# Order of the 64-row products in a four-layer graph network: lower rows first, then upper rows

## The chip, the core and the metric

The kernel runs on one core of a Trainium2 chip. A core has five engines with an instruction queue each: PE (TensorE, matrix products), DVE (VectorE), ACT (ScalarE), POOL (GpSimd) and SP (SyncE, which here only issues DMA transfers). They run side by side and wait for each other through semaphores. The metric is the device time of one execution in microseconds (us), lower is better.

## What is computed

The reference is four message-passing layers over one graph with 8,192 nodes, 32 features a node and 262,144 edges that are sorted by their target node. Each layer adds its result to the features and normalizes every node.

```python
x = layernorm(x + L0(x))     # msg = x[src] @ weight[edge_type]          (64 weights of 32x32)
x = layernorm(x + L1(x))     # msg = x[src] * edge_weight
x = layernorm(x + L2(x))     # msg = x[src]
x = layernorm(x + L3(x))     # h = relu(edge_attr_32 @ W1 + b1); w = h @ W2 + b2   (256 numbers an edge)
                             # msg = tensor product of x[src], edge_attr_4 and w
# in each layer: out = segment_sum(msg, dst)
```

## The kernel before

`raw_layers` writes its own order: each engine's instructions stand in the order of the Python loops, and waits are written out (`PE.after(mark)` makes PE's queue wait for a mark of another engine; `X.mark(ins)` sets one). No scheduler moves anything.

**Layer 0** first makes the table of x times all 64 weights in DRAM (L475). Then a loop over 256 groups `g` of 1,024 edges follows. POOL gathers the table rows of the edges, eight indirect DMAs a group, from `fetch_rows` through `indirect` (L454); it is let up to twelve groups ahead of PE (`AHEAD = 12`): the first half of group g+12 waits for PE's sums of g, the second half for all that PE has been given in g by then. DVE builds a one-hot matrix and splits the rows into three bfloat16 parts (`pairs`, `parts`; its first wait for a gather is at L858, its last step L863). PE then sums the group by target (L897).

In the same loop the kernel prepares layers 1 and 2: `matrices(i)`, 256 calls, 56 of the groups 8 to 207 with two calls and the others with one. Each call counts, for 128 nodes, which source blocks their edges come from, with and without the edge weight. DVE makes the one-hot operands `oh_k` and `oh_l` (L638, L640, L643) in two buffers, so that DVE's call i waits for PE's call i-2 (`oh_used`). PE then runs four rounds `q` of eight products (L654), and ACT empties each round with two copies (L658, L659). A round has its own two PSUM banks out of two pairs, so that round q waits for ACT's copies of round q-2 (`pair_free`). The operands of each product fill 64 of the 128 partitions: h = 0 the lower half, h = 1 the upper one. PE works with the rows of its array that belong to these partitions. The two halves write different PSUM banks.

The groups also run the first products of layer 1 (`layer1`, `products`, L717) as soon as counts and normalized nodes are there; `plan()` fixes at build time how many go into which group. None are planned before group 38. In the groups 8 to 207 it places 168; 100 of these 200 groups, 70 of the 170 from group 38 on, have none. `turn_back` (L736) and `add_up` (L752) finish a finished block of them; `normalize` with `windows` (L575) runs in groups 37, 69, 101, 133, 165, 197 and later ones.

**Layers 1 and 2** then run on the stored counts without gathers (L717, L1033).

**Layer 3** is a loop over 512 quads `q` of 512 edges. POOL gathers four times a quad, up to eight quads ahead (the gather of quad q+8 waits for PE's L1211 of quad q). PE's queue holds, for each quad: every second time the hidden layer (L1170, 32 rows), four products `h @ W2` (L1211, 64 rows each, added to biases that ACT wrote at L1190), and the summing of quad q-4 by target (L1221). DVE forms the messages (L1235 to L1256). Of the four products, `t` = 0 and 1 use the lower 64 rows and the first PSUM bank, `t` = 2 and 3 the upper rows and the second bank.

Every float32 product shows up in the profile as two weight loads and two passes: L654 has 256 x 4 x 8 = 8,192 products and 16,384 matmul records.

Of the kernel before, what the change touches and what calls it, by code (L numbers as in the profile page):

```python
# [161 lines left out]
def in_order(ctx: ExitStack, tc, x, a, w0, w1, b1, w2, si, keep):  # L162
# [36 lines left out]
    with tc.tile_critical():  # L199
        raw_layers(tc, x, a, w0, w1, b1, w2, si, m, bad)  # L200
# [3 lines left out]
def raw_layers(tc, x, a, w0, w1, b1, w2, si, m, bad):  # L204
# [35 lines left out]
    def now(f):  # L240
        return (f.sem, f.n)

    def own(f, ins):

        mk = f.mark(ins)
        f.after(mk)
        return mk
# [383 lines left out]
    def matrices(i):  # L631

        b, pp, k0 = i % 2, i // 2, 16 * (i % 2)
        if i % WB == 0:
            V.after(now(V))
            own(V, V.e.tensor_copy(w_ps, meta_w.rearrange("p n k -> p (n k)")[:, i * 16:(i + WB) * 16]))
        V.after(oh_used[b])
        own(V, V.e.tensor_tensor(oh_k[:, b, :, 0, :], iota2[:, None, 0:64, 0].to_broadcast([P, 16, 64]),  # L638
                                 meta_k[:, pp, k0:k0 + 16, None].to_broadcast([P, 16, 64]), op=OP.is_equal))
        V.e.tensor_tensor(oh_l[:, b], iota2[:, None, :, 0].to_broadcast([P, 16, P]),  # L640
                          meta_l[:, pp, k0:k0 + 16, None].to_broadcast([P, 16, P]), op=OP.is_equal)
        wo = (i % WB) * 16
        vm = V.mark(V.e.tensor_tensor(oh_k[:, b, :, 1, :], oh_k[:, b, :, 0, :],  # L643
                                      w_ps[:, wo:wo + 16, None].to_broadcast([P, 16, 64]), op=OP.mult))
        PE.after(vm)
        for q in range(4):
            u = units[0] % 2
            units[0] += 1
            PE.after(pair_free[u])
            two = bank[:, 2 + 2 * u:4 + 2 * u, :]  # L650
            for j in range(4):
                for h in range(2):
                    hs_ = slice(64 * h, 64 * h + 64)
                    ins = PE.e.matmul(two[:, h].rearrange("p (c s j) -> p c s j", s=64, j=4)[:, :, :, j],  # L654
                                      oh_l[hs_, b, 4 * q + j, :], oh_k[hs_, b, 4 * q + j], start=True, stop=True)
            pm = PE.mark(ins)
            A.after(pm, st_ld[b].mark() if q == 0 and st_ld[b].n else None)
            A.e.activation(st_c[:, b, q], two[:, :, 0:256], AF.Copy)  # L658
            pair_free[u] = am = A.mark(A.e.activation(  # L659
                st_a[:, b, :, q].rearrange("p z h w -> p h z w"),  # L660
                two[:, :, 256:512].rearrange("p h (z w) -> p h z w", w=32), AF.Copy))
        oh_used[b] = pm
        S.after(am)
        st_ld[b].add(S.e.dma_start(amat[i // 128][i // 8 % 16, :, 0:P * 2048].rearrange("z (p w) -> p z w", w=2048)[:, :, 256 * (i % 8):256 * (i % 8 + 1)],
                                   st_a[:, b].rearrange("p z q h w -> p z (q h w)")))
        stored[i] = st_ld[b].add(S.e.dma_start(cmat[i], st_c[:, b].rearrange("p u h c -> p (u h c)")))
# [174 lines left out]
    def fetch_rows(g, h, let):  # L841

        if g < GG:
            G.after(let)
            gathers(ytab, row, g * GT // WT, g * GT % WT + h * GT // 2, GT // 2)
            if h == 1:
                landed[g] = under_way[-1]
# [30 lines left out]
    for g in range(GG + 2):  # L878
# [9 lines left out]
        h, bk, c = g % NO, (g // per) % 2, g % per  # L888
# [13 lines left out]
        if g >= FIRST:  # L902
            upto = min(CB, (g - FIRST + 1) * CB // SP1)
            while made < upto:
                matrices(made)
                made += 1
# [293 lines left out]
    for q in range(NQ + LAG3 + 2):  # L1200
# [5 lines left out]
            hidden(q + 2)  # L1206
        if q < NQ:
            PE.after(quad[q]["h"], bm)
            for t in (0, 2, 1, 3):
                hp, c0 = slice(32 * (t & 2), 32 * (t & 2) + 64), 256 * (q % 2) + t % 2 * P  # L1210
                ins = PE.e.matmul(wp[:, t, :], hs[hp, q // 2 % 2, c0:c0 + P], w2_s[hp], start=False, stop=True,  # L1211
                                  skip_group_check=True)
            quad[q]["w"] = PE.mark(ins)
            quad[q]["k"] = k, wp
            fetch_rows(q + AHEAD)
# [545 lines left out]
```

## Time and profile before

| what | value |
|---|---|
| median of 14 runs | 5785.61 us (5780.81 to 5790.93) |
| the profiled execution | 5787.71 us, of which its span 5785.9 us |
| layer 0's table, until the first gather at 223.0 | 223 us |
| layer 0's gathers, 2,048, first to last start | 223.0 to 2803.6 us |
| `matrices` on PE (L654), first to last start | 359.9 to 2401.9 us |
| layers 1 and 2 on PE after the loop | about 2804 to 3186 us |
| layer 3's gathers, 2,048, first to last start | 3169.1 to 5738.9 us |
| `h @ W2` (L1211), first to last start | 3186.4 to 5752.5 us |
| mean granted PE clock over the span | 0.87 of full |

How to read it: the page gives each engine's busy time, then the span in 40 slices with the busy share in tenths, then groups of instructions with their count, busy time, mean duration and the idle time before them with what ended it. PE's row counts matmul passes, PEld the loads of weights that run beside them. PEclk is the clock that the throttle granted to PE, in tenths. A busy engine is not the one that sets the end unless somebody waits for it; the ends of matmuls are modelled, their starts are recorded.

### The profile page before, as it was taken

How to read it: one execution, taken by the hardware profiler on the slowest of the kernel's cores; microseconds unless marked ns; L12 is line 12 of the kernel's file. 1: busy time of each engine (PE TensorE's matmuls, PEld its weight loads, DVE VectorE, ACT ScalarE, POOL GpSimd, SP SyncE). 2: the span in 40 equal slices, each digit the busy share in tenths (PEclk: the TensorE clock that was granted, in tenths of full speed). 3: DMA queues.
4: the chain of work that ended last, by engine and by line, in shares of the span. 5: the costliest groups of instructions: out<-in, count | busy, mean ns of one | idle time of the engine just before them, and what ended most of it. 6: DMA issues, size and time to landing. Idle time of an engine off the chain costs nothing.

```text
span 5785.9 us, 89563 instructions
## 1 busy us (share of the span) xinstructions
PE 4549.5 (79%) x34750; PEld 2971.7 (51%) x34750; DVE 4399.7 (76%) x9506; ACT 2229.9 (39%) x3323; POOL 4141.7 (72%) x4236
## 2 busy tenths in 40 slices
PE   7456777778778788654599888889898888889897
PEld 3146666666666666432355444444444444444454
DVE  4269898989989898443355778878788878878786
ACT  5255555555555555210177222222222222222222
POOL 2677777777777777777356777777777777777775
PEclk7578888989999899756589899999999999999899
DMA  9636667769788899955576111111111111111111
GB/s 349 217 103 209 183 211 229 250 226 325 248 298 309 276 347 324 348 178 190 193 253 215 26 26 30 26 30 30 26 30 26 30 30 26 30 26 30 26 30 22
DMA packets 583331, 865.52 MB, mean 150 GB/s; under 512 B 102640, under 2 KB 441840, under 8 KB 549360
## 3 DMA queue, kind: packets, MB, share of 16 engines
q1 hardware_dynamic: 448320, 782.88, 38.5%
q0 software_dynamic: 134144, 73.67, 8.0%
q8 instruction: 276, 4.52, 0.3%
q10 hardware_dynamic: 432, 3.15, 0.2%
q14 instruction: 159, 1.30, 0.1%
HBM read 454.48 MB, written 404.88 MB: 149 GB/s over the span
## 4 chain that ended last, share of the span: by engine, by line
PE 18%; POOL 13%; DVE 8%; DMA 7%; issue 5%; ACT 1%; POOLq 0%; DVEq 0%
POOL f_arena L454 13%; DMA f_arena<-fxtab,f_src 7%; PE bank L1221 7%; PE bank L1033 4%; PE bank L1211 3%; DVE f_arena L1256 2%; PE bank L1170 1%; PE bank L717 1%; DVE f_arena L1252 1%; DVE f_arena L588 1%; ACT bank L1190 1%; PE bank L575 1%; PE bank L980 1%; DVE f_arena L1249 1%; DVE f_arena L1240 1%
## 5 line engine op out<-in xcount | busy, mean ns | idle before, releaser
L454 POOL DMA_INDIRECT f_arena<-fytab,f_row x2048 | 1957.7, 956 | 651.8 <-issue 549.5
L454 POOL DMA_INDIRECT f_arena<-fxtab,f_src x2048 | 1947.0, 951 | 643.4 <-issue 523.2
L654 PE MATMUL bank<-f_arena 64*128 64x128 f32 x16384 | 1208.7, 305 | 401.8 <-DVE f_arena L643 269.4
L1221 PE MATMUL bank<-f_arena 128*128 128x344 f32 x4096 | 1407.7, 488 | 0.0
L654 PEld LDWEIGHTS bank<-f_arena 64*128 64x128 f32 x16384 | 1111.2, 211 | 482.9 <-DVE f_arena L643 293.8
L1190 ACT ACTIVATE bank<-f_arena 128x1024 f32<-128x1024 f32 x512 | 526.5, 1029 | 1446.5 <-DVE f_arena L1256 1441.7
L1221 PEld LDWEIGHTS bank<-f_arena 128*128 128x128 f32 x4096 | 781.0, 201 | 531.0 <-issue 220.1
L658 ACT ACTIVATE f_arena<-bank 128x512 uint8<-128x512 f32 x1024 | 613.0, 599 | 844.9 <-PE bank L654 726.8
L1211 PE MATMUL bank<-f_arena 64*128 64x256 f32 x4096 | 621.4, 424 | 277.4 <-ACT bank L1190 276.7
L1211 PEld LDWEIGHTS bank<-f_arena 64*128 64x128 f32 x4096 | 370.8, 195 | 653.4 <-ACT bank L1190 471.3
L659 ACT ACTIVATE f_arena<-bank 128x512 f32<-128x512 f32 x1024 | 611.8, 597 | 0.0
L640 DVE TENSOR_TENSOR f_arena<-bank,f_arena 128x2048 f32<-128x2048 bf16 x256 | 586.6, 2291 | 8.7
L1256 DVE TENSOR_TENSOR f_arena<-bank,f_arena 128x256 f32<-128x256 f32 x1536 | 550.5, 413 | 0.0
L1134 DVE TENSOR_TENSOR f_arena<-f_arena 128x192 f32<-128x192 f32 x256 | 93.9, 367 | 396.9 <-DMA f_arena<-fxtab,f_src 395.8
L897 PE MATMUL bank<-f_arena 128*128 128x96 bf16 x2048 | 152.9, 227 | 305.8 <-DVE f_arena L863 305.8
L717 PE MATMUL bank<-f_arena,f_x_b 128*32 128x256 f32 x4096 | 327.3, 461 | 78.0 <-DMA f_arena<-famat 60.3
L588 DVE TENSOR_TENSOR f_arena<-bank,f_rel 128x512 f32<-128x512 f32 x512 | 348.6, 681 | 0.0
L1252 DVE TENSOR_TENSOR f_arena<-bank,f_arena 128x512 f32<-128x512 f32 x512 | 348.5, 681 | 0.0
L638 DVE TENSOR_TENSOR f_arena<-bank,f_arena 128x1024 f32<-128x1024 bf16 x256 | 312.0, 1219 | 15.1 <-PE bank L654 13.0
L897 PEld LDWEIGHTS bank<-f_arena 128*128 128x128 bf16 x2048 | 111.5, 108 | 388.9 <-DVE f_arena L863 299.4
L643 DVE TENSOR_TENSOR f_arena<-f_arena,bank 128x1024 f32<-128x1024 f32 x256 | 309.6, 1209 | 0.0
L1177 ACT ACTIVATE f_arena<-bank,f_arena 128x512 f32<-128x512 f32 x256 | 174.1, 680 | 336.6 <-PE bank L1170 336.3
(149 smaller groups left out, 4608.1 us busy)
## 6 DMA issues: line engine op xcount, KB each, us to landing
famat<-f_arena SPq DMA_DIRECT2D x256, 1024.0 KB
f_arena<-famat SPq DMA_DIRECT2D x256, 1024.0 KB, 6.6
fytab<-f_arena SPq DMA_DIRECT2D x64, 1024.0 KB, 11.9
fcmat<-f_arena SPq DMA_DIRECT2D x256, 256.0 KB
f_arena<-fcmat SPq DMA_DIRECT2D x16, 4096.0 KB, 14.7
f_arena<-fytab,f_row POOLq DMA_INDIRECT x2048
f_arena<-fxtab,f_src POOLq DMA_INDIRECT x2048
f_arena<-laid_ea SPq DMA_DIRECT2D x64, 512.0 KB
```

Source lines behind the costliest of these rows:

```text
L454: return G.e.indirect_dma_start(out=dest, out_offset=None, in_=table, in_offset=bass.IndirectOffsetOnAxis(ap=ix, axis=0))
L588: return V.e.tensor_tensor(o, iota[:, None, :].to_broadcast([P, n, P]), rel[:, t:t + n, None].to_broadcast([P, n, P]), op=OP.is_equal)
L640: V.e.tensor_tensor(oh_l[:, b], iota2[:, None, :, 0].to_broadcast([P, 16, P]), meta_l[:, pp, k0:k0 + 16, None].to_broadcast([P, 16, P]), o ...
L654: ins = PE.e.matmul(two[:, h].rearrange("p (c s j) -> p c s j", s=64, j=4)[:, :, :, j], oh_l[hs_, b, 4 * q + j, :], oh_k[hs_, b, 4 * q + j ...
L658: A.e.activation(st_c[:, b, q], two[:, :, 0:256], AF.Copy)
L659: pair_free[u] = am = A.mark(A.e.activation(st_a[:, b, :, q].rearrange("p z h w -> p h z w"), two[:, :, 256:512].rearrange("p h (z w) -> p ...
L717: ins = PE.e.matmul(acc[q * D:(q + 1) * D, :].rearrange("p (u h j) -> p u h j", h=2, j=4), x_b[:, 8 * z + s, :], mv[:, s], start=(first an ...
L1190: return A.mark(A.e.activation(wp, b2_s[:, None, :].to_broadcast([P, 4, 256]), AF.Copy))
L1211: ins = PE.e.matmul(wp[:, t, :], hs[hp, q // 2 % 2, c0:c0 + P], w2_s[hp], start=False, stop=True, skip_group_check=True)
L1221: ins = PE.e.matmul(bank[:, g % 2, 0:MW], oh[:, c % NO, t, :], p[:, c % NP, t, :], start=(c % 2 == 0 and t == 0), stop=(c % 2 == 1 and t = ...
L1252: V.e.tensor_tensor(pq[:, :, 0:128].rearrange("p t (o k) -> p t o k", k=16), wp[:, :, 0:128].rearrange("p t (o k) -> p t o k", k=16), a0[: ...
L1256: ins = V.e.tensor_tensor(pq[:, :, 128 + 64 * mm:192 + 64 * mm].rearrange("p t (o i) -> p t o i", i=8), wp[:, :, 192:256].rearrange("p t ( ...
```

## The change

Both places keep the same products, operands and PSUM banks; only their order on PE's queue differs. In `matrices`, the loop over the halves becomes the outer one: the four products on the lower 64 rows run first, then the four on the upper 64. In layer 3 the order of the four products goes from lower, upper, lower, upper to lower, lower, upper, upper.

```diff
@@ matrices
-            for j in range(4):
-                for h in range(2):
+            for h in range(2):
+                for j in range(4):
                     hs_ = slice(64 * h, 64 * h + 64)
                     ins = PE.e.matmul(two[:, h].rearrange("p (c s j) -> p c s j", s=64, j=4)[:, :, :, j],
                                       oh_l[hs_, b, 4 * q + j, :], oh_k[hs_, b, 4 * q + j], start=True, stop=True)
@@ layer 3
             PE.after(quad[q]["h"], bm)
-            for t in (0, 2, 1, 3):
+            for t in range(4):
                 hp, c0 = slice(32 * (t & 2), 32 * (t & 2) + 64), 256 * (q % 2) + t % 2 * P
                 ins = PE.e.matmul(wp[:, t, :], hs[hp, q // 2 % 2, c0:c0 + P], w2_s[hp], start=False, stop=True,
                                   skip_group_check=True)
```

## The prediction

> **What bounds the kernel now.** I read the page's engine rows and slices first, then the groups, then for both loops a stretch of the timeline in order of time.
>
> ```profile
> span 5785.9 us, 89563 instructions
> PE 4549.5 (79%) x34750; PEld 2971.7 (51%) x34750; DVE 4399.7 (76%) x9506; ACT 2229.9 (39%) x3323; POOL 4141.7 (72%) x4236
> ...
> PEclk7578888989999899756589899999999999999899
> ...
> L454 POOL DMA_INDIRECT f_arena<-fytab,f_row x2048 | 1957.7, 956 | 651.8 <-issue 549.5
> L454 POOL DMA_INDIRECT f_arena<-fxtab,f_src x2048 | 1947.0, 951 | 643.4 <-issue 523.2
> L654 PE MATMUL bank<-f_arena 64*128 64x128 f32 x16384 | 1208.7, 305 | 401.8 <-DVE f_arena L643 269.4
> ```
>
> The two gather streams set both loops: 2,048 gathers at 0.956 us plus some 0.3 us of issue are 2,580 us each, and the first runs from 223.0 to 2803.6, the second from 3169.1 to 5738.9. Mean spacing is 1.26 us, so POOL gives 10.0 us to a group of layer 0 (eight gathers) and 10.0 us to two quads of layer 3. PE, DVE and ACT follow it with some idle time. So the change costs what PE cannot hide under 10.0 us a group or a pair of quads.
>
> Where PE stands in the loops:
>
> ```profile
> 1254.89 2.14 PE L654 MATMUL bank<-f_arena 64*128 64x128 f32 x32 [0.29 <-ACT f_arena L659]
> 1256.97 0.51 PE L897 MATMUL bank<-f_arena 128*128 128x96 bf16 x8
> 1257.65 2.06 PE L654 MATMUL bank<-f_arena 64*128 64x128 f32 x32 [0.16 <-DVE f_arena L643]
> ```
>
> ```profile
> 4580.49 2.59 PE L1221 MATMUL bank<-f_arena 128*128 128x344 f32 x8
> 4583.01 1.07 PE L1170 MATMUL bank<-f_arena 32*64 32x512 f32 x4
> 4584.01 1.13 PE L1211 MATMUL bank<-f_arena 64*128 64x256 f32 x8
> 4585.08 2.59 PE L1221 MATMUL bank<-f_arena 128*128 128x344 f32 x8
> 4587.59 1.13 PE L1211 MATMUL bank<-f_arena 64*128 64x256 f32 x8
> 4588.66 2.59 PE L1221 MATMUL bank<-f_arena 128*128 128x344 f32 x8
> ```
>
> The reader is to see that 32 passes of L654 (two rounds) take 2.06 us although one pass lasts 0.27: a lower and an upper pass start 7 ns apart and run together, and the next pair starts 0.112 us later (0.213 at half clock). Rounds follow each other at 0.995 us, at half clock at 1.71. In layer 3 one L1211 block holds PE for 1.07 us, again in pairs (0.213 us each), and a pair of quads takes 4588.66 - 4580.49 = 8.17 us when PE never waits.
>
> **The clock.** The slices show it at 7 to 9 tenths. What it follows can be read in stretches:
>
> ```profile
> core 0: us, PE busy (x), PEclk, DMA share, GB/s
> 357.30:364.10 6.80, 4.21 (x38) 0.50 0.10 13
> 364.10:374.30 10.20, 7.01 (x109) 1.00 0.50 145
> 36.60:60.40 23.80, 22.90 (x72) 0.50 1.04 389
> 111.70:118.50 6.80, 6.80 (x34) 1.00 0.84 302
> 3186.00:5786.00 2600.00, 2273.07 (x9338) 0.94 0.15 28
> ```
>
> The two stretches at 36.60 and 111.70 hold only L475: passes of 32 rows and 512 columns. In both PE looks busy throughout, yet the first stays at half clock. A pass at full clock streams its 512 columns in 512/128 x 0.107 = 0.43 us (0.112 less 5 ns of start) on 32/128 of the array. So the array's work is 72 x 0.43 / 4 / 23.8 = 0.33 of its capacity in the first, 34 x 0.43 / 4 / 6.8 = 0.54 in the second. Weighted this way, by rows and columns in use, the clock's steps (3.4 us long) over the whole trace divide at about 0.37: steps below it are followed by half clock, steps above it by full clock, with some ten exceptions in 1,680. By time busy alone the L475 rows contradict. That matters here: alternating, L654 has work 0.107/0.112 = 0.96 at full and 0.49 at half clock, so it lifts the clock by itself (364.10 above). With one half at a time it has about half of that.
>
> **The change, part by part.** No instruction is added or removed; waits, banks and DMAs stay. What goes is the overlap of the halves.
>
> *One round of L654.* [...] Before, 8 pairs span 7 pitches; after, 14. Added: 7 x 0.112 = 0.78 us (1.49 at half clock). A round takes 1.78 (3.20), more than ACT's two copies at 0.60 each, so ACT stops ending PE's waits. A call of four rounds takes 7.1 us on PE at full clock, 13.0 at half (12.8 and 0.2 to start).
>
> [...]
>
> *Its work rate.* 16 passes x 0.107 x 1/2 = 0.85 us of the whole array in 1.78 us is 0.48; at half clock, in 3.20 us, 0.27. At full clock that stays above 0.37 if PE idles less than 0.8 us of a 3.4 us step. At half clock it can't climb; only full-array work in the same step can, of which products L717 (0.97 us each, near 0.9 of the array) are the supply: some 2 us of them at half clock must fall into one step.
>
> *Layer 0, groups 8 to 37* (355 to 658 us, 303 us; 38 calls). No L717 is planned and the clock is at half on entry. I expect it stays there: 38 x 13.0 + 30 x (0.82 for L897 + 0.3) = 528 us: **+225**. Bound below: full clock, 38 x 7.1 + 30 x 0.8 = 294, hidden: 0.
>
> *Groups 38 to 207* (658 to 2404 us, 1,746 us; 218 calls, 168 products). At full clock: 218 x 7.12 = 1,552; 168 x 0.97 = 163; 170 sums x 0.52 = 88; 106 turns (L736) x 0.63 = 67; five normalizations x 10 (6.5 us waiting for L863, and L575) = 50. PE has 1,920 us of work: **+174**, since POOL's 10.0 us a group no longer covers it.
>
> *Half clock in those groups.* Every group at half costs 1.28 calls x 5.9 + 0.6 = 8.1 us more. 70 of the 170 groups have no product to lift the clock; waits that drop it (five normalizations, 34 waits of ACT L658 for a store of `fcmat`) remain. I take 45 groups: **+366**. Bounds: 0, and all 170, +1,380.
>
> *What POOL's lead gives back.* At group 208 PE is now 70 us behind the gathers (2404 against 2335). It can be 12 groups x 10.3 = 123 us: 54 us are absorbed, **-54**. Groups 208 to 255 stay at POOL's pace, as before.
>
> *Queued behind it.* ACT's L658 and DVE's L638 (`oh_used`) wait for L654, and POOL's second half group for all of PE's calls; DVE has at most two calls of one-hots ready, so it slows to PE's pace but adds nothing: 9.4 us a group (3.2 for L583 and the parts, 1.28 x 4.7, 0.14).
>
> *Layer 3.* Four pairs (3 pitches) become 6 pitches: 3 x 0.213 = 0.64 us a quad; a pair of quads 8.17 + 1.28 = 9.45 us under POOL's 10.0, still covered. What isn't: eight normalizations keep PE from quads for some 14 us each, and the clock is at half for 336 of 2,600 us, which costs PE 168 us. 256 x 9.45 + 8 x 14 = 2,531, with those 168 us 2,699, against 2,570: between 0 and +130. Half-clock steps come from idle steps, which get fewer as PE fills: **+40**.
>
> **Sum:** 225 + 174 + 366 - 54 + 40 = 751 over the span of 5785.9 (its execution 5787.7, within 0.04% of the median 5785.6): **6537 us**.
>
> **Rivals.**
> *The clock stays up* (the gate counts time busy, or 0.48 is enough everywhere). [...] For it: L475 at 111.70 keeps full clock at 0.54. Against: 36.60. Terms: 0 + 174 + 0 - 54 + 20 = +140: 5926 us.
> *The clock stays down nearly everywhere.* For: once down, L654 can't lift it. Against: 100 groups with products. 225 + 174 + 1,380 - 54 + 130 = +1,855: 7641 us. With three quarters of the groups, 7296.
> *Not slower.* Gathers hide it all. PE's call would have to take at most (1,746 + 54 - 368) / 218 = 6.6 us, a round 1.64 instead of 1.78, so one pair in six would still have to overlap, and the clock to stay up. Then 5786 within 10. [...]
>
> **How the numbers follow.** Forecast 0.68, clock up 0.12, clock down nearly everywhere 0.15, not slower 0.05. The forecast's own range is 6170 (no half groups from 38 on) to 7000 (100 of them). For 8 in 10 the range goes from 5950, inside the first rival, to 7350, inside the second. A measurement tells about 0.2% (12 us) from no change: faster 0.02, same 0.03, slower 0.95.
>
> **What would show it.** L654 passes in one half 0.112 us apart, a round of 1.78 or 3.20 us; groups 8 to 37 at clock 0.5 taking some 530 us; half clock in layer 0 rising from 443 us to near 1,000; POOL waiting for L654; layer 3's gathers still near 2,570 us. Wrong if the clock in layer 0 stays near 0.9, if a round stays near 1.0, or if layer 3 grows by more than 130.

## The result, and the profile after

The changed kernel takes 5838.79 us (median of 6 runs, 5836.31 to 5844.52), the kernel before 5784.9 (28 runs): a ratio of 1.0094, 95% interval 1.0084 to 1.0104, some 54 us slower. The forecast was 6537, with a range from 5950: the sign was right, the size was not. The profiled execution of the changed kernel is 27 us above its median (5865.5, span 5863.7), so its differences to the trace before add up to 78 us, not 54.

From the page of the changed kernel:

```profile
span 5863.7 us, 89563 instructions
PE 4870.1 (83%) x34750; PEld 3315.3 (57%) x34750; DVE 4399.7 (75%) x9506; ACT 2270.0 (39%) x3323; POOL 4150.6 (71%) x4236
...
PEclk7578998989889899866579899999999999999998
...
L454 POOL DMA_INDIRECT f_arena<-fytab,f_row x2048 | 1960.7, 957 | 718.2 <-issue 549.5
L454 POOL DMA_INDIRECT f_arena<-fxtab,f_src x2048 | 1952.8, 954 | 643.4 <-issue 520.6
L654 PE MATMUL bank<-f_arena 64*128 64x128 f32 x16384 | 1542.9, 300 | 189.9 <-DVE f_arena L643 115.0
```

L654 is busy 334 us longer (1208.7 before), and idle 212 us less ahead of it (401.8). POOL's first gather stream idles 66 us more (651.8), the second not at all: the loss lies in layer 0. The slices show no fall of the clock. Stretches of PE in layer 0, groups 8 to 37 and 38 to 207, first before, then after (columns: stretch, length, PE busy, clock, DMA share, GB/s):

```profile
355.00:658.00 303.00, 207.54 (x2680) 0.84 0.61 185
658.00:2404.00 1746.00, 1347.85 (x18542) 0.90 0.83 278
```

```profile
357.00:663.00 306.00, 258.58 (x2688) 0.87 0.60 183
663.00:2501.00 1838.00, 1619.80 (x18526) 0.93 0.79 264
```

The clock is a little higher than before, the groups from 38 on take 92 us more. What one round costs now shows in the timeline of the changed kernel; before, the same 32 passes took 2.06 us:

```profile
1202.63 2.82 PE L654 MATMUL bank<-f_arena 64*128 64x128 f32 x32 [0.17 <-DVE f_arena L643]
```

By their recorded starts at full clock, a round's first upper pass begins together with the fifth of the eight lower passes, 0.55 us after the first, and its last upper pass 1.44 us after the first lower one (0.89 before). Where nothing holds the next round, it does not wait for that last pass: its first lower pass starts together with the fifth upper pass, ahead of the three upper ones that are left, 1.11 us after the first lower pass of the round before (0.995 in the kernel before; 1.78 forecast). The third round waits for ACT's copies of the first and begins 1.45 us after the first round's last pass in both kernels. As that pass now comes later, the third round begins 2.88 us after the first (2.35 before).

A call of four rounds lasts 5.70 us at full clock instead of 4.49 (7.1 forecast). Of these 1.21 us, 0.11 each lie between the starts of the first and second and of the third and fourth round, 0.43 between those of the second and third, and 0.56 in the last round itself.

Summed over the 256 calls that is 1331 us before and 1612 after, 281 more. In the groups 8 to 207 (2049 us before, 2144 after) the time outside the calls falls from 718 to 532: 186 of the 281 us went into time in which PE had waited anyway, 95 remained. At group 208 PE is 146 us behind the gathers instead of 69. POOL's lead hides little of this in the end: PE comes to group 208 97 us later than before, and the last gather of layer 0 starts 71 us later. Who waited for L654 in the changed kernel, in us and times:

```profile
  ACT f_arena L658: 819.3, 566
  POOL f_arena L454: 70.9, 74
```

POOL waited 20.4 us before: of the 71 us, 50 are POOL standing at the gate to the next group because PE had not got through its calls. POOL's waits from 2345 us on, when it fetches group 208 (total, times, longest):

```profile
POOL f_arena L454 <- PE bank L654: 35.0, 7, 12.5
POOL f_arena L454 <- PE bank L897: 20.6, 9, 11.8
```

No gather of layer 0 starts over 1.5 us after the one before it ended in the kernel before. In the changed kernel ten do: two in groups 177 and 180, 15 us together, and eight in groups 209 to 222, 52 us together. So the loss comes out where POOL reaches its gate.

Layer 3 of the changed kernel:

```profile
4304.57 1.07 PE L1170 MATMUL bank<-f_arena 32*64 32x512 f32 x4
4305.57 1.14 PE L1211 MATMUL bank<-f_arena 64*128 64x256 f32 x8
4306.64 2.59 PE L1221 MATMUL bank<-f_arena 128*128 128x344 f32 x8
```

L1211 holds PE for 1.07 us, as before. The starts of its eight passes (0, 13, 321, 333, 538, 551, 753, 766 ns) are nearly those of the alternating order (0, 6, 321, 326, 538, 544, 753, 759): with two products to a half, the upper half begins 13 ns after the lower one.

### The profile page after: what moved, and what is told of

The parts are those of the page before. It is cut to its first block, busy times and chain, and to the rows that moved or that the text cites. A ratio compares the mean times of both kernels' runs of the same rounds, so it can differ in the third digit from the quotient of the medians.

```text
span 5863.7 us, 89563 instructions
## 1 busy us (share of the span) xinstructions
PE 4870.1 (83%) x34750; PEld 3315.3 (57%) x34750; DVE 4399.7 (75%) x9506; ACT 2270.0 (39%) x3323; POOL 4150.6 (71%) x4236
## 4 chain that ended last, share of the span: by engine, by line
PE 16%; POOL 13%; DVE 8%; DMA 7%; issue 5%; ACT 1%; POOLq 0%; DVEq 0%
POOL f_arena L454 13%; DMA f_arena<-fxtab,f_src 7%; PE bank L1221 6%; PE bank L1033 4%; PE bank L1211 3%; DVE f_arena L1256 2%; PE bank L1170 1%; DVE f_arena L1252 1%; DVE f_arena L588 1%; ACT bank L1190 1%; PE bank L717 1%; PE bank L980 1%; PE bank L575 1%; DVE f_arena L1249 1%; DVE f_arena L1240 1%
## 5 line engine op out<-in xcount | busy, mean ns | idle before, releaser
L654 PE MATMUL bank<-f_arena 64*128 64x128 f32 x16384 | 1542.9, 300 | 189.9 <-DVE f_arena L643 115.0
L654 PEld LDWEIGHTS bank<-f_arena 64*128 64x128 f32 x16384 | 1452.3, 201 | 261.0 <-DVE f_arena L643 127.5
L658 ACT ACTIVATE f_arena<-bank 128x512 uint8<-128x512 f32 x1024 | 611.7, 597 | 916.5 <-PE bank L654 819.3
L1211 PE MATMUL bank<-f_arena 64*128 64x256 f32 x4096 | 618.1, 420 | 284.8 <-ACT bank L1190 284.1
L1211 PEld LDWEIGHTS bank<-f_arena 64*128 64x128 f32 x4096 | 377.7, 194 | 652.8 <-ACT bank L1190 482.3
L659 ACT ACTIVATE f_arena<-bank 128x512 f32<-128x512 f32 x1024 | 606.3, 592 | 0.0
L643 DVE TENSOR_TENSOR f_arena<-f_arena,bank 128x1024 f32<-128x1024 f32 x256 | 309.6, 1210 | 0.0
```

The lines of the kernel that those rows point to most:

```text
L659: pair_free[u] = am = A.mark(A.e.activation(st_a[:, b, :, q].rearrange("p z h w -> p h z w"), two[:, :, 256:512].rearrange("p h (z w) -> p ...
```

## The experiments

The question was why the halves still overlap, and where the 54 us come from. The theory after the result (A) was my reading of the starts in the changed kernel's trace: the upper half begins with the fifth of eight lower passes in L654 and with the first of four in L1211, so each time three lower passes still wait; if that is the most that can, only a run of more than four passes on one half loses anything. The expectations below give 1.33 us between rounds. That is where the seventeenth pass of a call starts in order of time; since the rounds overlap, it is not the first of the next round, which starts after 1.11 us. Rivals: strict program order (B), a loss in layer 3 (C), and causes other than PE's time. On the chips of e1 to e4, e9 to e11 and e12 the kernel of before itself took 7383 to 7433 us, so their ratios hold for those chips alone; e5 to e8 ran where it took 5778.

**One part alone.**

```diff
# e1, e9: layer 3 alone
-            for t in (0, 2, 1, 3):
+            for t in range(4):
```

> Only the order of the four products of 64 rows in layer 3 is changed (lower, lower, upper, upper). Theory A (PE starts a pass on the other rows although up to three passes on the first rows still wait; only longer runs on one half lose anything): a half has two products, four passes, so the first upper pass starts 10 ns after the first lower one, as before; time 5785, within 0.2%. Theory B (passes start strictly in program order, only the last lower and the first upper one overlap, as I predicted): one block of four products takes 1.70 us instead of 1.06, PE 9.45 us per pair of quads, time 5785 to 5830. Theory C (the loss of the whole change comes from layer 3): 5839.

> Only layer 3's order is changed, once more beside the next run on one chip. A run of 64 rows is four passes long, and the first upper pass starts 10 ns after the first lower one in the trace of the whole change too: 1.000 of before, within 0.2%.

Measured: 1.000 (0.999 to 1.001) and 1.000 (0.9989 to 1.0011). C falls; layer 3's order costs nothing, though on these chips POOL doesn't set layer 3's pace alone (layer 3's gathers take 3,025 us in e9).

```diff
# e2, e10, e12: matrices alone
-            for j in range(4):
-                for h in range(2):
+            for h in range(2):
+                for j in range(4):
```

> Only the order in the matrices of layer 0 is changed (four products on the lower rows, then four on the upper). Theory A: the whole loss is here: 5839, within 0.2% of the whole change; rounds of L654 1.33 us apart at full clock instead of 0.995. Theory C (the loss comes from layer 3): 5785.

> Only the order in layer 0's matrices is changed, once more. All of the loss of the whole change: 1.0094 of before, within 0.2%, a call of the matrices 5.70 us at full clock.

> Only the order in layer 0's matrices is changed, a third time, in case this chip runs the kernel of before in 5785: 1.0094 of before, within 0.2%, all of the loss of the whole change; a call of the matrices 5.70 us at full clock, 1.21 more than before. If part of the loss came from layer 3's order, it is smaller by that part.

Measured: 1.0227 (1.0206 to 1.0248), 1.0224 (1.0202 to 1.0246) and 1.0248 (1.0218 to 1.0279). Where nothing holds a round, the next follows 1.11 us later, as in the whole change, but the ratio is not the expected 1.0094. On these chips POOL waits for L654 already without this edit (e9: waiting engine and line, what it waited for, total, times, longest):

```profile
POOL f_arena L454 <- PE bank L654: 761.3, 129, 12.3
ACT f_arena L658 <- remote: 758.6, 168, 54.8
```

L654 is on the path there, so the same longer round costs more. The whole change was not run on such a chip; that all of its loss is layer 0's rests on e1 and e9 and on layer 3's nearly equal starts and gathers (2,570 us before, 2,576 after, first to last start; 2,574 in e5 with the old order there, 2,572 in e8 with the new one).

**How many passes still wait when the other half starts.** In e11 three pairs of long runs stand ahead of layer 0's loop, on lines of their own, between products of all rows (L833):

```diff
+    for _ in range(8):
+        PE.e.matmul(bank[:, 2, 0:P], ident[lo], shift[lo, 0:P], start=True, stop=True)      # L836
+    for _ in range(8):
+        PE.e.matmul(bank[:, 3, 0:P], ident[up], shift[up, 0:P], start=True, stop=True)      # L838
...
```

L841 and L843 are the same with 320 columns, L846 and L848 have 16 products a half of bfloat16 with 256 columns.

> Kernel of before, and ahead of the loop of layer 0, where PE is idle, three pairs of long runs between products of all rows: 8 products on the lower 64 rows, then 8 on the upper, each kind on a line of its own: float32 of 128 columns (16 passes a half), float32 of 320 columns (16 passes), bfloat16 of 256 columns (16 products, one pass each). If PE looks past a fixed number of waiting passes, the first upper pass starts with the lower pass number 13 of 16 in all three, whatever a pass takes. If it looks a fixed time ahead (0.33 us, three passes of 0.112), it starts with number 13 for 128 columns and about number 15 for 320. If passes start strictly in program order, after number 16 in all.

The first pair in e11's timeline (at half clock):

```profile
231.11 3.14 PE L836 MATMUL bank<-f_shift,f_ident 64*128 64x128 f32 x13
233.84 0.58 PE L838 MATMUL bank<-f_shift,f_ident 64*128 64x128 f32 x1
234.05 0.42 PE L836 MATMUL bank<-f_shift,f_ident 64*128 64x128 f32 x1
234.22 0.42 PE L838 MATMUL bank<-f_shift,f_ident 64*128 64x128 f32 x1
234.26 0.42 PE L836 MATMUL bank<-f_shift,f_ident 64*128 64x128 f32 x1
234.43 0.42 PE L838 MATMUL bank<-f_shift,f_ident 64*128 64x128 f32 x1
234.47 0.42 PE L836 MATMUL bank<-f_shift,f_ident 64*128 64x128 f32 x1
234.64 2.98 PE L838 MATMUL bank<-f_shift,f_ident 64*128 64x128 f32 x13
```

Thirteen lower passes start, then an upper one, 6 ns after the thirteenth, and only then lower 14, 15 and 16, in turn with upper ones. In all three kinds the first upper pass starts with lower pass 13 of 16, although a pass takes 0.213 us in the first and third and 0.533 in the second. So in this run three lower passes still wait when the first upper one starts, with the shorter and with the longer pass: the same number and not the same time, and B falls.

**Runs short enough.**

```diff
# e3, e5
-            for j in range(4):
-                for h in range(2):
+            for j2, h in ((0, 0), (0, 1), (1, 0), (1, 1)):
+                for j in (2 * j2, 2 * j2 + 1):
```

> The matrices of layer 0 in runs of two products: lower, lower, upper, upper, lower, lower, upper, upper; layer 3 as before. Theory A (up to three waiting passes are looked past): runs of four passes lose nothing: rounds 0.995 us apart, time 5785 within 0.2%. Theory B (program order): the three changes of half overlap by one pass each, 3 + 3 + 3 + 3 pitches and one overlap more than in the whole change: a round of about 1.45 us, PE longer than with the whole change as it measured, so at least 5839.

> The matrices of layer 0 in runs of two products (lower, lower, upper, upper, lower, lower, upper, upper), once more, in case this chip runs the kernel of before in 5785. If up to three waiting passes of one half are looked past, rounds are 0.995 us apart and the time is that of before within 0.2%; if the loss of the change came from leaving the strict alternation at all, some 0.9% slower like the whole change.

Measured: e5 0.9995 (0.9985 to 1.0004), rounds 0.995 us apart. Two rounds in e5's timeline (2.06 us before, 2.82 in the changed kernel):

```profile
1199.71 2.16 PE L654 MATMUL bank<-f_arena 64*128 64x128 f32 x32 [0.77 <-DVE f_arena L643]
```

So runs of four passes on one half cost the kernel nothing here. A call is not quite as short as with strict turns: a round's last pass starts 0.10 us later, and a call lasts 4.68 us at full clock in e5, against 4.49. On the chip of e3 the rounds are 0.995 apart too and the ratio is 1.0034 (1.002 to 1.0047), a little over the 0.2% I had allowed; the longer call fits, but what the 0.3% are was not tried.

**No overlap at all.** What the forecast took the change to do:

```diff
# e4, e6: the counts of the upper 64 partitions are left out
-            for j in range(4):
-                for h in range(2):
-                    hs_ = slice(64 * h, 64 * h + 64)
+            for h in range(2):
+                for j in range(4):
+                    hs_ = slice(0, 64)
```

> All eight products of a round use the lower 64 rows (the counts of the upper half of the partitions are left out and those of the lower half written twice), so no two passes can run together: what I had predicted the change would do. A round should take 16 pitches: 1.78 us at full clock, 3.4 at half clock. If the clock follows the share of the array at work (0.48 at full clock, 0.25 at half, threshold 0.37): groups 8 to 37 stay at half clock and take some 530 us instead of 303, half clock in layer 0 is several hundred us more than before, time 6200 to 7000, about 6540. If the clock follows how long PE is busy at all: full clock nearly throughout layer 0, time 5900 to 5960.

> All eight products of a round on the lower 64 rows (the counts of the upper half of the partitions are left out), once more, in case this chip runs the kernel of before in 5785. Clock by share of the array at work: rounds 1.79 us apart at full clock and 3.41 at half, groups 8 to 37 at half clock all through, most of layer 0 too; 30 groups at 20 us and up to 170 at 19 instead of 10 are +300 and up to +1,500: 7000 to 7600. Clock by time busy: 5900 to 5960.

Measured: e4 8495.8, 1.144 (1.1409 to 1.1465); e6 6681.8, 1.156 (1.1519 to 1.1608). Rounds are 1.786 us apart at full clock and 3.413 at half. e6, groups 8 to 37 and 38 to 207 (columns as above), and one call in the first stretch:

```profile
356.00:927.00 571.00, 555.72 (x2684) 0.50 0.34 100
927.00:3353.00 2426.00, 2321.00 (x18538) 0.81 0.61 200
```

```profile
505.92 14.02 PE L654 MATMUL bank<-f_arena 64*128 64x128 f32 x64
```

PE is busy for 556 of 571 us and the clock is at half for 568 of them. So time busy did not bring the full clock in this stretch. The share of the array at work is 0.25 by estimate (16 passes of 0.107 us on half the array in 3.41), below the 0.37 at which the clock's steps divide in the trace of before. My expectation of 7000 to 7600 was too high, that of the forecast, 6537, within 2.2%: in groups 38 to 207, where products of layer 1 run too, the mean clock is 0.81, and 930 of the 2,426 us are at half.

**The same PE time with the halves overlapping.**

```diff
# e7
-            for j in range(4):
+            for j in (0, 1, 2, 3) + (3,) * (1 + q % 2):
                 for h in range(2):
```

> Order of before, but the last pair of products is repeated: once in even rounds, twice in odd ones, 1.5 pairs a round, 3 x 0.112 = 0.336 us more of PE with the halves overlapping (the results stay the same). If the loss of the change is nothing but PE time in the rounds (1.33 instead of 0.995 us), the time is that of the whole change: +0.9% (5840) within 0.3%. If it comes from something else in the new order (passes of two halves colliding with ACT's copies, the clock), clearly less, near 5785.

Measured: 5794.3, 1.0029 (1.0019 to 1.0039): 16 us, not 55. By the expectation that speaks against the passes' time as the only cause, but the added time was not the same either. A call takes 5.52 us at full clock, 0.18 less than the changed kernel's, and the clock is higher: in groups 8 to 207 it is at half for 242 us, against 348 in the changed kernel and 443 before. The calls add up to 1539 us instead of 1612. By estimate the shorter call is worth 256 x 0.18 = 46 us and the 107 us less at half clock within the calls some 53; together that is more than the 73, so how they divide stays open. PE comes to group 208 46 us later than in the trace before, 97 in the changed kernel; the last gather starts 20 and 71 us later, so some 26 us are absorbed in both. So the loss follows how late PE is, and the clock is part of that. That the added passes, with both halves at work, lift the clock and so pay part of their own time back is my estimate from these times at half clock; it was not tried alone.

**More lead.**

```diff
# e8, on top of the change
-    AHEAD = 12
+    AHEAD = 15
```

> The whole change, with POOL allowed 15 groups ahead instead of 12. If PE is the slower one in groups 8 to 207 and the time appears only where POOL's lead is used up, three groups more of lead hide up to 3 x 10 us: 5805 to 5820, and POOL's wait for L654 falls from 71 us to some 40. If POOL's gate is not on the path: 5839.

Measured: 5802.0, 1.0047 (1.003 to 1.0064), half of the loss gone, and POOL waits 36.5 us for L654. The last gather of layer 0 starts at 2826 instead of 2875 us. PE comes to group 208 79 us later than in the trace before, and the last gather starts 22 us later: 56 us absorbed instead of 26, three groups of 10 us more. This confirms where the time comes out: at POOL's gate, once its lead is used up. No version here beats the kernel before; it keeps POOL gathering nearly without a break, and the runs of two only equal it.

## Why the prediction was wrong

- **What bounds the kernel: right.** POOL's gathers set both loops. They show the loss, and a longer lead takes half of it away (e8).
- **One round: the step that failed.** It took 7 more pitches, 1.78 us a round and 7.1 a call. No run shows these 7 pitches for the changed order; only e4 and e6, with all products on one half, have rounds 1.786 us apart. Measured in the changed kernel: the first upper pass starts with the fifth lower one and not with the eighth, the next round's first lower pass with the fifth upper one, and a call takes 5.70, 1.21 more than before where the forecast added 4 x 0.78 = 3.1. Three passes on one half still wait at each of these starts, as they do in e11. The alternating trace held a first sign: the upper product's first pass starts 7 ns after the lower one's first, 0.1 to 0.2 us ahead of the lower one's second. If a product's two passes follow each other on the queue, as I take it, one pass was waiting there. How many can, that trace could not show. The same step had "ACT stops ending PE's waits": the third round of a call still waits for ACT's copies of the first, and PE sits idle 61 us for L659 (125 before).
- **Work rate and clock: right in kind, without an occasion.** With four rounds in 5.70 us the array's share over a call is 4 x 0.85 / 5.70 = 0.60 by estimate, well above the 0.37 read from the trace of before. Weighted by rows and columns in use, the clock's steps divide near 0.37 in the traces of the changed kernel, e6 and e7 too, with 17 to 28 exceptions in 1,700 to 1,960 steps. In groups 8 to 37 the clock was at half for 82 us (98 before), in 38 to 207 for 266 (345). So the terms +225 and +366 fell away: the first was +2. The forecast's premise, rounds of 1.78 us, is met in e6: rounds 1.786 us apart, groups 8 to 37 at half clock for 568 of 571 us, and 6682 us, against 6537. There groups 8 to 37 took 572 us (528 forecast), groups 38 to 207 2,425 (2,286), POOL's lead gave back 26 (54), layer 3 cost 3 (40).
- **Groups 38 to 207 at full clock: mis-sized twice.** With 5.70 us a call the same sum would be 218 x 5.70 + 368 = 1,611, under POOL's 1,746, and thus hidden; measured was +93. PE's work is no bound that it reaches: in groups 8 to 207 it still idles 266 us (494 before), for DVE's one-hots at L643 (115), ACT's L659 (61) and the parts at L863 (43) above all, while others are full. This is also why the rival "not slower" failed, although both of its conditions held (a call under 6.6 us, the clock up).
- **POOL's lead: right in kind, mis-sized.** At group 208 PE is 77 us further behind the gathers, but POOL then stands at its gate until group 222. From PE's 97 us at group 208 to the 71 us of the last gather only 26 were absorbed, not 54; the forecast's "groups 208 to 255 stay at POOL's pace, as before" did not hold.
- **Layer 3: +40 forecast, measured about +6** over its gathers, hardly more than versions with the old order differ (3 to 4 us in e5, e6 and e7); its runs of four passes lose no overlap: eight starts span 766 ns, 759 in the alternating order. No run shows the 3 pitches a quad that the forecast added.
- **The change does what it says**, in both places; in layer 3 nothing follows from it.

## What to carry to other kernels

Products on separate row halves did not have to alternate strictly here: with runs of four passes on one half (two float32 products) rounds stayed 0.995 us apart, and only a round's last pass started 0.10 us later (e5). With runs of eight, in the changed kernel, the other half began with the fifth pass, and of the 1.21 us that a call lost 0.43 lay at the wait for ACT's copies and 0.56 in the last round. Before costing a lost overlap, look for a stretch of the trace that has the order in question, or measure it in an idle corner of the kernel; the alternating order, with the halves 7 ns apart, did not show how many passes may still wait. And an engine that "fits" under the bound by its sum of work can still show part of a longer step, since its waits for others don't all give way (186 of 281 us did here), and what a lead seems to absorb can come out later where its gate closes.

## What the hardware showed that I had not expected

- Passes start out of program order across row halves in e11: three lower passes of 16 still wait when the first upper one starts, with passes of 0.213 and of 0.533 us, in float32 and bfloat16 alike.
- The clock stayed at half for 568 of 571 us while PE was busy for 556 of them, with half of the array's rows in use (e6). Here the clock went with the share of the array at work, 0.25 by estimate, and not with the time busy.
- Twelve runs fell on chips of two kinds: on some the unchanged kernel takes 5778 to 5785 us, on others 7383 to 7433, with the same gather (0.956 us) and copy times. There engines wait long for nothing that the trace shows, as ACT's L658 above ("remote", 758.6 us in e9). What it is stays open.
